# Mamba scan: where the kept state's column is added to the next slot's first column

## The chip, the cores and the metric

One Trainium2 chip, one of its cores. The metric is the device time of one execution in microseconds; several executions are timed and the median is given. The engines named here are TensorE (PE; PEld are its weight loads), VectorE (DVE), ScalarE (ACT), GpSimd (POOL) and SyncE (SP, which issues DMAs). They run side by side, each through its own instructions in order, and wait for one another by semaphores.

## What is computed

The network has two layers on a map of 64 x 64 positions with 256 channels, all in float32: first convolutions with an attention over channels and heads, then a bidirectional Mamba block with a small MLP, then a layer of eight experts of which two are used. The change lies in the Mamba block alone. Cut to it:

```python
# per direction; x: (1, 4096, 256), DI = 512 channels, DS = 16 states
xz = einsum('bld,ed->ble', x, in_proj_w);  xc, z = split(xz, 2)
xc = silu(causal_conv4(xc) + conv_b)
x_dbl = einsum('bld,ed->ble', xc, x_proj_w)      # dt (16), B (16), C (16)
dt = softplus(einsum('blr,dr->bld', dt, dt_proj_w) + dt_proj_b)
A = -exp(A_log)
dA = exp(dt[..., None] * A)                      # decay
dBx = dt[..., None] * Bm[:, :, None, :] * xc[..., None]   # inflow

def step(h, inp):
    dA_t, dBx_t, C_t = inp
    h = dA_t * h + dBx_t                         # 512 x 16 states, position after position
    return h, einsum('bds,bs->bd', h, C_t)

y = (scan(step) + xc * Dp) * silu(z)
return einsum('bld,ed->ble', y, out_proj_w)
```

The block runs forward and on the reversed sequence; the two results are added, and a layer norm with an MLP follows.

## The kernel before

**Phases.** The program runs convolutions, attention, Mamba and experts one after the other (lines 2296 to 2301). The Mamba phase goes from about 1.9 ms to 3.8 ms of the profile.

**Chunks and slots.** The 4096 positions are cut into 8 chunks of N = 512. With two directions that makes 16 passes i (chunk i // 2, direction i % 2; the directions alternate). A pass has SPS = 32 slots: 4 channel tiles e, 4 groups of states k, and j in (0, 2). A slot handles 64 channels times 4 states on 128 partitions (32 channels x 4 states), in two halves v that lie one behind the other in a tile of 128 x 1024. `slots` lists all 512 of them in order (L1871).

**What a slot does.** ScalarE makes the decay dA of both halves into a tile `da` in PSUM (`decay`, L1886, two activations of 512). GpSimd makes the inflow `dbx` in SBUF (`inflow`, L1896). VectorE runs h = dA * h + dBx along all 1024 columns in one instruction (`recur`, L1909), whose first value comes from the kept state, and then multiplies the result by C (L1914). In five slots of a pass (POOLED = 4, 10, 12, 18, 28) the scan writes to SBUF, and GpSimd does that product (`pooled`, L1919). ScalarE copies the last column of each half to the kept state (`keep`, L1940). TensorE sums over the states (`sum_states`, L1949).

**Two halves in one scan.** The second half holds other channels, so what the first half leaves must not run into it. For that the first column of dt of these channels is made huge (L1475), so that the decay there is zero. What their own kept state should have given is added to the first column of the second half of `dbx` instead. `carry` makes these values ahead of time, once for each half of a pass: `brought` = exp(A * dt of the first position) * state (L1493 on GpSimd, L1495 on ScalarE, L1498 on GpSimd; its four parts stand at slots 30, 31, 9 and 11 and the exponentials at 30 and 10). `bring` adds one column of `brought` to one column of `dbx` (128 x 1). The passes i = 0 and 1 start from zero and have nothing to bring, so this concerns 448 slots.

**Who brings.** `bring(n, True)` stands in `inflow` for the slots 1, 9, 17 and 24 of a pass (LONG) and runs on GpSimd (L1932, 56 of them). The others are done by ScalarE (L1934, 392 of them): `bring(n + 1)` stands in the loop ahead of `recur(n)`, behind `decay(n + 1)`. The set `there` keeps a slot from being done twice.

**Order.** The loop over the slots (L1985 to L2047) writes out the order of every engine's instructions by hand (`tc.manual_schedule`); what stands first in the loop stands first in each queue. In the round of slot n: a part of `carry`, `inflow(n + 2)`, `keep(n - 1)`, `decay(n + 1)`, `bring(n + 1)`, `recur(n)`, then loads of later tiles by SyncE, `pooled(n - 1)`, the sums over states, and a step of the work beside it: the next pass's projections (`prepare`), the output projection, and the layer norm and MLP of a finished chunk (`tail`: L1554, L149 on GpSimd; L129, L1568, L1578, L1585 on VectorE). There are three buffers for `dbx`, two for `da` and four for `h`, so GpSimd's inflow of a slot starts when the scan three slots before it has ended.

Of the kernel before, what the change touches and what calls it, by code (L numbers as in the profile page):

```python
# [18 lines left out]
AF = mybir.ActivationFunctionType  # L19
ALU = mybir.AluOpType  # L20
# [41 lines left out]
def step(gen, n=1):  # L62

    for _ in range(n):
        if gen is None or next(gen, StopIteration) is StopIteration:
            return False
    return True
# [1188 lines left out]
def mamba_phase(cx, early, w_in, w_x, w_out, w1, w2, x1d, ud, bcd, dtd, x2d, u2d, usum):  # L1256
# [11 lines left out]
    nc, tc = cx.nc, cx.tc  # L1268
    with ExitStack() as ctx:
# [60 lines left out]
        def exp_and_log():  # L1330
            nc.scalar.preload_act_table_set("natural_log_exp_and_others")
# [153 lines left out]
        def carry(q, h, part):  # L1485


            tiles = slice(2 * h, 2 * h + 2)
            if part == 0:
                x = brought[q, h] = ip.tile([P, 2, 2, SQ], FP, name="brought", tag="in")  # L1490
                first = got_first.pop((q, h)).rearrange("p (a b) e -> p e a b", b=2)[:, :, :, 1]
                a = aneg[q % 2].rearrange("p (e a b k) -> p e a b k", e=ET, a=2, b=2)[:, tiles, :, 1, :]
                nc.gpsimd.tensor_tensor(x, a, first[..., None].to_broadcast([P, 2, 2, SQ]), ALU.mult)  # L1493
            elif part == 1:
                nc.scalar.activation(brought[q, h], brought[q, h], AF.Exp)  # L1495
            else:
                old = state[q % 2].rearrange("p (e a b) k -> p e a b k", a=2, b=2)[:, tiles, :, 1, :]
                nc.gpsimd.tensor_tensor(brought[q, h], brought[q, h], old, ALU.mult)  # L1498
# [367 lines left out]
        def slab(n):  # L1866
# [4 lines left out]
        slots = [  # L1871
            (i, e, k, j) for i in range(2 * NCH) for e in range(ET) for k in range(SQ) for j in (0, 2)
        ]
        SPS = ET * SQ * 2
        firsts, first_rows, got_first, brought = {}, {}, {}, {}
        gots, bcs, dts, m_of, das, us, ys, hs = {}, {}, {}, {}, {}, {}, {}, {}

        def decay(n):

            if n >= len(slots):  # L1880
                return
            i, e, k, j = slots[n]
            da = das[n] = pda.tile([P, 2, N], FP, name="da", tag="da")
            for v in range(2):
                a = SQ * (4 * e + j + v) + k
                nc.scalar.activation(  # L1886
                    da[:, v, :], dts[i, e, j][0][:, v, :], AF.Exp, scale=aneg[i % 2][:, a : a + 1]
                )

        def inflow(n):  # L1890

            if n >= len(slots):
                return
            i, e, k, j = slots[n]
            u = us[n] = up.tile([P, 2, N], FP, name="dbx", tag="dbx")
            nc.gpsimd.tensor_tensor(  # L1896
                u, dts[i, e, j][1], bcs[i, k][0][:, None, :].to_broadcast([P, 2, N]), ALU.mult
            )
            if n % SPS in LONG:
                bring(n, True)  # L1900

        def recur(n):

            i, e, k, j = slots[n]
            da, u = das[n], us.pop(n)
            h = hs[n] = hp.tile([P, 2, N], FP, name="h", tag="h")
            if n % SPS in POOLED:
                das[n] = h
            nc.vector.tensor_tensor_scan(  # L1909
                das[n].rearrange("p v n -> p (v n)"), da.rearrange("p v n -> p (v n)"),  # L1910
                u.rearrange("p v n -> p (v n)"), state[i % 2][:, 4 * e + j, k : k + 1], ALU.mult, ALU.add,
            )
            if n % SPS not in POOLED:
                nc.vector.tensor_tensor(h, da, bcs[i, k][1][:, None, :].to_broadcast([P, 2, N]), ALU.mult)  # L1914

        def pooled(n):

            i, e, k, j = slots[n]
            nc.gpsimd.tensor_tensor(hs[n], hs[n], bcs[i, k][1][:, None, :].to_broadcast([P, 2, N]), ALU.mult)  # L1919

        def bring(n, pool=False):


            if n >= len(slots) or n in there:
                return
            there.add(n)
            i, e, k, j = slots[n]
            if i < 2:
                return
            x, old = us[n][:, 1, 0:1], brought[i, e // 2][:, e % 2, j // 2, k : k + 1]  # L1930
            if pool:
                nc.gpsimd.tensor_tensor(x, x, old, ALU.add)  # L1932
            else:
                nc.scalar.activation(x, x, AF.Identity, bias=old)  # L1934

        def keep(n):

            i, e, k, j = slots[n]
            g = 4 * e + j
            nc.scalar.copy(state[i % 2][:, g : g + 2, k], das.pop(n)[:, :, N - 1])  # L1940
# [16 lines left out]
            g, z = gots[i]["xc"], gots[i]["z"]  # L1957
            nc.vector.tensor_tensor(g[:, e, :], ys.pop((i, e)), z[e // 2][:, e % 2, :], ALU.mult)

        there = set()  # L1960
        CARRY = {30: (0, 0), 31: (0, 2), 9: (1, 0), 11: (1, 2)}


# [2 lines left out]
        AHEAD = 5  # L1966

        LATE = {0: 0, 1: 0, 2: 0, 3: 0, 5: 2, 6: 2, 7: 5, 15: 2, 16: 2, 17: 2}
        LONG = {1, 9, 17, 24}

        FULL = {
            "PE": {0, 1, 2, 3, 4, 5, 6, 7, 9, 18, 19, 20, 21, 23, 24, 25, 27, 29},
# [6 lines left out]
        with tc.manual_schedule(engines=ORDERED):  # L1979
            gots[0] = {"u": early.u}  # L1980
            begin = start()
            step(begin)
            coming = prepare(1)
            tails, prep, out, last = [], None, None, None
            for n, (i, e, k, j) in enumerate(slots):  # L1985
                at = n % SPS
                if at == 0:
                    prep, coming = coming, None
                if at in CARRY and 1 < i + (at > 16) < 2 * NCH:
                    carry(i + (at > 16), *CARRY[at])  # L1990
                inflow(n + 2)
                if n > 0:
                    keep(n - 1)
                if n > 0:
                    decay(n + 1)
                bring(n + 1)
                recur(n)
                nxt = (i, e + 1) if e < ET - 1 else (i + 1, 0)
                if nxt[0] < 2 * NCH:
                    if e == ET - 1 and j == 0:  # L2000
                        load_bc(i + 1, k)
                    if (k, j) == (1, 2):
                        load_dt(*nxt, 0)
                    if (k, j) == (2, 2):
                        load_dt(*nxt, 2)
                if n > 0 and (n - 1) % SPS in POOLED:
                    pooled(n - 1)
                if j == 2 and n > 2 and (n - 3) % SPS in POOLED:
                    sum_states(n - 3)
                if j == 0 and n > 0:  # L2010
                    if (n - 2) % SPS not in POOLED:
                        sum_states(n - 2)
                    if k == 0:
                        close(*slots[n - 2][:2])
                        if e == 0:
                            out = output(i - 1)
                if 1 <= at <= 3 and out is not None:
                    step(out)
                    if at == 3:
                        out = None  # L2020
                        if (i - 1) % 2:
                            tails.append(tail((i - 1) // 2))
                if at == 0 and i > 0:
                    for z in gots[i]["z"]:
                        nc.scalar.activation(z, z, AF.Silu)
                    exp_and_log()
                if i == 0:
                    step(begin)
                step(prep, LATE.get(at, 1) if i == 0 else 1)
                if at >= SPS - AHEAD and i + 2 < 2 * NCH:  # L2030
                    coming = coming or prepare(i + 2)
                    step(coming)
                if i > 0 and at in (2, 4):
                    dt_piece(i, 1, 2 if at == 2 else 3)
                if at == 1 and i > 1:
                    load_first(i, 1)
                elif at in (10, 30) and 1 < i + (at > 16) < 2 * NCH:
                    carry(i + (at > 16), at < 16, 1)
                if i == 2 * NCH - 1 and at in (4, 5, 6, 7, 10, 11, 12, 13, 15, 17, 19, 21, 23, 25, 27, 28, 29, 30):
                    last = last or ahead()  # L2040
                    step(last)
                for _ in range(1 + (i == 2 * NCH - 1 and at in (4, 6, 7))):
                    if tails and (i == 2 * NCH - 1 or at not in FULL[needs[0]]):
                        needs[0] = next(tails[0], None)
                        if needs[0] is None:
                            tails.pop(0)
                            needs[0] = "PE"  # L2047
            ending()
# [357 lines left out]
```

## Time and profile before

| | us |
|---|---|
| median of 3 runs | 4104.75 (4104.18 to 4105.28) |
| the profiled execution | 4093.77 |
| its span, first to last instruction | 4091.8 |
| busy: PE / DVE / ACT / POOL | 3572.0 / 3502.8 / 2628.2 / 1837.9 |
| mean granted clock of TensorE | 0.928 |

The instructions that bring, and those that make what they bring (mean duration, ns):

| line, engine | count | mean | busy us |
|---|---|---|---|
| L1934 ACT, adds the column | 392 | 280 | 109.9 |
| L1932 POOL, adds the column | 56 | 189 | 10.6 |
| L1493 POOL | 28 | 222 | 6.2 |
| L1495 ACT | 28 | 213 | 6.0 |
| L1498 POOL | 28 | 222 | 6.2 |
| L1940 ACT, keeps the state | 511 | 160 to 186 | 83.7 |

How to read the lines of the profile: a group has its line, engine and operation, what it writes and reads by the program's names, shapes (partitions x elements), the count; then busy us and mean ns of one; then the idle time of the engine just before them and what ended most of it. In a timeline the first number is the start in us from the span's start, the second the duration. Starts matter more than durations there: an instruction can start before the one ahead of it on its engine has ended.

### The profile page before, as it was taken

The page shows a single profiled execution, that of the slowest core. Times are in us where ns is not written, and L with a number is a line of the kernel's source. Part 1 is how long each engine was busy: PE and PEld are TensorE (multiplying, and loading weights), DVE is VectorE, ACT ScalarE, POOL GpSimd, SP SyncE. Part 2 cuts the span into 40 slices and gives each one's busy share as a digit, 9 for nine tenths or more (in the row PEclk, how much of TensorE's full clock was granted, in tenths as well). Part 3 has the DMA queues.
Part 4 walks back from the last instruction along what each step waited for, and adds up shares of the span by engine and source line. Part 5 has one row for each costly group of instructions (what it writes and reads, how often), then busy time and mean ns, then how long its engine had stood idle before and what let it go on. Part 6 is the DMA issues. An engine that isn't in the chain of part 4 may idle for free. (4 is left out here: it accounts for less than half of the span.)

```text
span 4091.8 us, 43210 instructions
## 1 busy us (share of the span) xinstructions
PE 3572.0 (87%) x14792; PEld 1173.9 (29%) x14792; DVE 3502.8 (86%) x2919; ACT 2628.2 (64%) x4118; POOL 1837.9 (45%) x1284
## 2 busy tenths in 40 slices
PE   6769988999999999998788888888888888876898
PEld 2324332222222222222222222222222232222444
DVE  8998877989889889877899999999999999999322
ACT  1111236988888888875777777777787777775222
POOL 3020000000000000001888889989888989888100
PEclk9879998999999999998888899999889899888999
DMA  6232214223223222214334444344334444432111
GB/s 209 94 101 92 79 62 152 57 55 71 63 55 65 64 59 61 58 42 126 119 105 130 114 126 132 119 127 122 119 109 122 142 110 133 123 118 93 62 62 55
DMA packets 164324, 399.93 MB, mean 98 GB/s; under 512 B 36997, under 2 KB 46469, under 8 KB 163838
## 3 DMA queue, kind: packets, MB, share of 16 engines
q1 hardware_dynamic: 137166, 304.26, 24.4%
q0 software_dynamic: 24624, 84.43, 8.9%
q10 hardware_dynamic: 2304, 8.39, 0.6%
q8 instruction: 118, 1.93, 0.2%
q14 instruction: 112, 0.92, 0.1%
HBM read 268.17 MB, written 79.56 MB: 85 GB/s over the span
## 5 line engine op out<-in xcount | busy, mean ns | idle before, releaser
L1896 POOL TENSOR_TENSOR dbx<-dtxr,b 128x1024 f32<-128x1024 f32 x512 | 1202.8, 2359 | 192.6 <-DVE da L1909 89.6
L1044 ACT ACTIVATE e<-sc 128x1024 f32<-128x1024 f32 x1024 | 993.8, 1023 | 168.1 <-PE sc L1037 144.0
L1909 DVE TENSOR_TENSOR_SCAN da<-da,state,dbx 128x1024 f32<-128x1024 f32 x432 | 1013.8, 2347 | 16.4 <-ACT da L1886 7.0
L954 DVE TENSOR_TENSOR s<-s,e 128x1024 f32<-128x1024 f32 x768 | 880.2, 1216 | 18.7 <-ACT e L1044 18.0
L1886 ACT ACTIVATE da<-dtr,aneg 128x512 f32<-128x512 f32 x1024 | 708.1, 692 | 33.6 <-DMA dtr<-dtd 3.1
L1037 PE MATMUL sc<-q,kS 32*128 32x512 f32 x4096 | 648.2, 645 | 15.7 <-ACT e L1044 11.4
L1914 DVE TENSOR_TENSOR h<-da,c 128x1024 f32<-128x1024 f32 x432 | 529.0, 1225 | 32.1 <-DVE da L1909 0.5
L961 PE MATMUL av<-e,vT 128*32 128x512 f32 x4096 | 552.3, 608 | 0.1
L977 POOL DMA_DIRECT2D s<-s x94 | 81.5, 874 | 943.4 <-DVE s L954 872.8
L1949 PE MATMUL y<-h,sel 128*32 128x512 f32 x2048 | 374.6, 661 | 96.3 <-DVE h L1914 72.8
L462 PE MATMUL cv<-v,u 128*128 128x512 f32 x928 | 413.8, 606 | 27.5 <-DVE pad L283 14.2
L1037 PEld LDWEIGHTS sc<-q,kS 32*128 32x128 f32 x4096 | 211.2, 184 | 456.1 <-issue 256.2
L1342 PE MATMUL mm<-u,win 128*128 128x512 f32 x464 | 242.8, 665 | 71.2 <-ACT z L1450 30.0
L1940 ACT COPY state<-da 128x2 f32<-128x2 f32 x431 | 68.8, 160 | 292.0 <-DVE h L1914 288.2
L462 PEld LDWEIGHTS cv<-v,u 128*128 128x128 f32 x928 | 179.2, 195 | 260.2 <-issue 227.5
L560 DVE SCALAR_TENSOR_TENSOR acc<-pad,wdw_s,acc 128x768 f32<-128x768 f32 (+1 forms) x192 | 235.9, 1234 | 19.9 <-ACT acc L553 14.2
L143 POOL TENSOR_TENSOR ln_few<-ln_few,minus_half 128x4 f32<-128x4 f32 x29 | 36.2, 1249 | 397.6 <-DMA ln_few<-ln_row 260.2
L1388 PE MATMUL mm<-xp,taps 128*128 128x512 f32 x480 | 213.3, 596 | 0.5 <-DVE m L1538 0.5
L954 DVE TENSOR_TENSOR s<-e 128x1024 f32<-128x1024 f32 x128 | 151.8, 1217 | 60.7 <-ACT e L1044 60.5
L1909 DVE TENSOR_TENSOR_SCAN h<-da,state,dbx 128x1024 f32<-128x1024 f32 x80 | 187.5, 2344 | 10.8 <-ACT state L1940 9.8
L961 PEld LDWEIGHTS av<-e,vT 128*32 128x32 f32 x4096 | 81.9, 108 | 394.3 <-issue 385.9
L1919 POOL TENSOR_TENSOR h<-h,c 128x1024 f32<-128x1024 f32 x80 | 188.4, 2355 | 1.0 <-ACT state L1940 1.0
(375 smaller groups left out, 3887.0 us busy)
## 6 DMA issues: line engine op xcount, KB each, us to landing
dtr<-dtd SPq DMA_DIRECT2D x128, 512.0 KB
dtxr<-dtd SPq DMA_DIRECT2D x128, 512.0 KB
s<-s POOLq DMA_DIRECT2D x94, 512.0 KB, 6.0
b<-bcd SPq DMA_DIRECT2D x64, 256.0 KB
c<-bcd SPq DMA_DIRECT2D x64, 256.0 KB
dtd<-dt SPq DMA_DIRECT2D x64, 256.0 KB
dtd<-few SPq DMA_DIRECT2D x64, 256.0 KB
u<-uv SPq DMA_DIRECT2D x24, 640.0 KB
```

What stands on the lines that cost most here:

```text
L462: nc.tensor.matmul(rows4(ps), u[:, dy, P * ci : P * ci + P], v[:, dy : dy + HR, ci, :], start=dy + ci == 0, stop=dy == k - 1 and ci == CT - 1,
L560: nc.vector.scalar_tensor_tensor(o, src, w_ap, o, ALU.mult, ALU.add)
L954: nc.vector.tensor_tensor(z, x, y, ALU.add)
L961: nc.tensor.matmul(g.av[32 * h : 32 * h + 32, :], vT[:, kb, P * t + 32 * h : P * t + 32 * h + 32], es[h // 2][:, h % 2, :], start=kb == 0, ...
L1037: nc.tensor.matmul(ps[h // 2][:, h % 2, :], kS[r, t, P * kb : P * kb + P], q_t[r, t, :], start=True, stop=True,)
L1044: nc.scalar.activation(e, ps[i], AF.Exp)
L1342: nc.tensor.matmul(ps, win[d][:, t, P * e : P * e + P], u[:, t, ::-1] if d else u[:, t, :], start=t == 0, stop=t == CT - 1,)
L1886: nc.scalar.activation(da[:, v, :], dts[i, e, j][0][:, v, :], AF.Exp, scale=aneg[i % 2][:, a : a + 1])
L1896: nc.gpsimd.tensor_tensor(u, dts[i, e, j][1], bcs[i, k][0][:, None, :].to_broadcast([P, 2, N]), ALU.mult)
L1909: nc.vector.tensor_tensor_scan(das[n].rearrange("p v n -> p (v n)"), da.rearrange("p v n -> p (v n)"), u.rearrange("p v n -> p (v n)"), st ...
L1914: nc.vector.tensor_tensor(h, da, bcs[i, k][1][:, None, :].to_broadcast([P, 2, N]), ALU.mult)
L1949: nc.tensor.matmul(ys[i, e][32 * j : 32 * j + 32, :], cx.sel, hs[n + j // 2][:, j % 2, :], start=False, stop=k == SQ - 1,)
```

## The change

All additions of the kept state's column go to VectorE. `bring(n + 1)` is now called inside `recur(n)`, behind the scan of slot n and ahead of its product, as a tensor_scalar with the column of `brought` as its per-partition scalar. It is no longer called in `inflow` and in the loop; `LONG` and `there` are gone. The passes 0 and 1 are left out as before, now by the number of the slot.

```diff
@@ inflow(n)
                 u, dts[i, e, j][1], bcs[i, k][0][:, None, :].to_broadcast([P, 2, N]), ALU.mult
             )
-            if n % SPS in LONG:
-                bring(n, True)
@@ recur(n)
                 u.rearrange("p v n -> p (v n)"), state[i % 2][:, 4 * e + j, k : k + 1], ALU.mult, ALU.add,
             )
+            bring(n + 1)
             if n % SPS not in POOLED:
                 nc.vector.tensor_tensor(h, da, bcs[i, k][1][:, None, :].to_broadcast([P, 2, N]), ALU.mult)
@@
-        def bring(n, pool=False):
+        def bring(n):
-            if n >= len(slots) or n in there:
+            if n >= len(slots) or n < 2 * SPS:
                 return
-            there.add(n)
             i, e, k, j = slots[n]
-            if i < 2:
-                return
-            x, old = us[n][:, 1, 0:1], brought[i, e // 2][:, e % 2, j // 2, k : k + 1]
-            if pool:
-                nc.gpsimd.tensor_tensor(x, x, old, ALU.add)
-            else:
-                nc.scalar.activation(x, x, AF.Identity, bias=old)
+            x = us[n][:, 1, 0:1]
+            nc.vector.tensor_scalar(x, x, brought[i, e // 2][:, e % 2, j // 2, k : k + 1], None, ALU.add)
@@
-        there = set()
-        LONG = {1, 9, 17, 24}
@@ the loop over the slots
                     decay(n + 1)
-                bring(n + 1)
                 recur(n)
```

## The prediction

> **What bounds the kernel now.** I read the totals of the page first, then the busy time of each engine in the stretch that the change touches (the 448 slots that bring a state, 2165 to 3800 us), then VectorE's waits in it, and then the timeline of VectorE instruction by instruction. These are the groups of the page and the row of the stretch (columns of the second: length, busy us of PE, PEld, DVE, ACT, POOL, clock, DMA):
>
> ```profile
> L1896 POOL TENSOR_TENSOR dbx<-dtxr,b 128x1024 f32<-128x1024 f32 x512 | 1202.8, 2359 | 192.6 <-DVE da L1909 89.6
> L1909 DVE TENSOR_TENSOR_SCAN da<-da,state,dbx 128x1024 f32<-128x1024 f32 x432 | 1013.8, 2347 | 16.4 <-ACT da L1886 7.0
> L1914 DVE TENSOR_TENSOR h<-da,c 128x1024 f32<-128x1024 f32 x432 | 529.0, 1225 | 32.1 <-DVE da L1909 0.5
> ...
> 2165.00:3800.00 1635.00, 1362.22 (x3856) 439.34 (x3856) 1575.77 (x963) 1226.94 (x2431) 1430.72 (x875) 0.90 0.40 119
> ```
>
> VectorE is busy for 1575.8 of 1635 us (96%), GpSimd 88%, TensorE 83%, ScalarE 75%. VectorE sets the pace; each microsecond that it gains or loses here moves everything behind, since the expert phase starts from the last chunk. What it waits for in the stretch (us in total, times, longest):
>
> ```profile
> DVE h L1909 <- ACT state L1940: 9.8, 13, 1.6
> DVE da L1909 <- ACT state L1940: 4.6, 8, 1.0
> DVE da L1909 <- ACT dbx L1934: 3.0, 6, 1.0
> DVE da L1909 <- POOL dbx L1932: 1.0, 1, 1.0
> ```
>
> So the scans lose 18.4 us in 28 places to ScalarE and GpSimd, and only 4.0 of that to the instruction that moves (L1934 and L1932). That is nearly all there is to gain.
>
> **What is removed and added.** ScalarE loses 392 activations (0.28 us each, 109.9 us; it gets back about 0.20 us start to start), GpSimd loses 56 additions (0.19 us, 10.6 us). VectorE gains 448 additions of one column, 378 behind a scan that a product follows, 70 (slots 4, 10, 12, 18, 28 of the 14 later chunks) behind a scan whose product is GpSimd's. No DMA is added or moved. What VectorE's timeline shows between its instructions (start, duration):
>
> ```profile
> 2642.07 2.34 DVE L1909 TENSOR_TENSOR_SCAN h<-da,state,dbx 128x1024 f32<-128x1024 f32 x1
> 2644.33 2.33 DVE L1909 TENSOR_TENSOR_SCAN da<-da,state,dbx 128x1024 f32<-128x1024 f32 x1
> 2646.70 1.23 DVE L1914 TENSOR_TENSOR h<-da,c 128x1024 f32<-128x1024 f32 x1
> 2647.84 2.35 DVE L1909 TENSOR_TENSOR_SCAN da<-da,state,dbx 128x1024 f32<-128x1024 f32 x1
> ```
>
> An instruction that does not need the scan's result starts 2.26 us after the scan's start (2642.07 to 2644.33, before the scan has ended). The product needs the result and starts 2.36 to 2.39 us after it in 182 of the 432 pairs and 2.42 to 2.46 in 249 (2.45 where it has a second semaphore to wait for, as at 2614.16 and 2616.61). So 0.12 to 0.19 us of the pipe are free between scan and product. The price of the new instruction is not in the stretch; its nearest row is a one-element tensor_scalar with a scalar read from SBUF, in the router:
>
> ```profile
> 3837.81 0.15 DVE L2085 TENSOR_SCALAR tw<-slab 128x1 f32<-128x1 f32 x1
> 3837.88 0.20 DVE L2086 TENSOR_SCALAR tw<-tw,slab 128x1 f32<-128x1 f32 x1
> 3838.00 0.86 DVE L169 TENSOR_SCALAR diag<-ident,ln_few 128x128 f32<-128x128 f32 x4
> ```
>
> It lasts 0.20 us, and the next one starts 0.12 after it.
>
> 1. *The 378 slots with a product.* 2.26 + 0.12 = 2.38: the addition fits in front of the product. Cost 0 to 0.12 each, 0 to 45 us; I take 2 us, as sum and row meet almost exactly. The cover is the product's own wait for the scan; without it, the 45 us would show.
>
> 2. *The 70 slots without a product.* Here the next scan reads the column that was just added. In 54 of them it is the next instruction, today 2.26 us after the scan. After the change: addition at 2.26, its end 0.20 later, and the dependent start 0.10 after that (a scan that waits for ScalarE as well has two semaphores, as the product at 2.45). 54 x 0.31 = 16.7 us; bounds 0.24 (one semaphore, 0.034 gap) and 0.12 if nothing waits: 6 to 17. In 16 of them a tail instruction (L129, L1568, L1578) stands between and only the 0.12 counts: 1.9 us.
>
> 3. *The wait that VectorE now takes itself.* The addition needs GpSimd's dbx of the next slot, and stands in VectorE's queue in front of the product, which does not need it; behind the product are the next scan, ScalarE's copy of the state, the decay into the PSUM buffer and TensorE's sums. Before, ScalarE took that wait:
>
> ```profile
> L1934 ACT ACTIVATE dbx<-dbx,brought x392: 277/279/297, 2165.0 to 3792.0; 128x1 f32<-128x1 f32 x196
> ...
>   POOL dbx L1896: 16.0, 23
> ```
>
> 23 times it stood waiting, while VectorE had a 1.14 us product to do. One such place:
>
> ```profile
> 2563.61 2.35 DVE L1909 TENSOR_TENSOR_SCAN da<-da,state,dbx 128x1024 f32<-128x1024 f32 x1
> 2566.07 1.23 DVE L1914 TENSOR_TENSOR h<-da,c 128x1024 f32<-128x1024 f32 x1
> 2567.21 0.74 DVE L1568 SCALAR_TENSOR_TENSOR a1a<-tl,small,a1a 128x512 f32<-128x512 f32 x1
> 2567.97 2.36 DVE L1909 TENSOR_TENSOR_SCAN da<-da,state,dbx 128x1024 f32<-128x1024 f32 x1
> ...
> 2565.26 4.66 POOL L1896 TENSOR_TENSOR dbx<-dtxr,b 128x1024 f32<-128x1024 f32 x2
> ```
>
> The first of GpSimd's two products, for the scan at 2567.97, ends at 2567.60. VectorE would reach the addition at 2563.61 + 2.26 = 2565.87 and stand for 1.77 us; the product moves from 2566.07 to about 2567.76. I compared each slot's scan start + 2.26 with the end of the matching GpSimd product (and of the chunk's L1498): late in 25 places. Neighbours counted once at the longest, and 0.98 us that one scan waits already taken off: 14.6 us. Most lie behind slots 4, 10 and 12, which step 2 makes longer by 0.31 each while GpSimd goes on; that takes off 0.6 to 0.9 in six of them. I take 10 (5 to 15). What is late next is nothing on GpSimd: it waits 76.0 + 15.4 us for scans elsewhere.
>
> 4. *Gains.* The 4.0 us of waits for the moved instruction go. The 21 waits for L1940 (14.4 us) stand behind decays that a ScalarE addition may have delayed by 0.20: at most 4.2, I take 3. GpSimd's 10.6 us lie beside VectorE's work and bring nothing.
>
> Sum: 2 + 16.7 + 1.9 + 10 - 4 - 3 = **+23.6 us**. The profiled execution takes 4093.77 us (span 4091.8, 2.0 around it), so 4117.4; the median of the runs shown, 4104.75, is 11 us (0.27%) above that execution, and I add to the median: **4128 us**.
>
> **A rival of large price: the two engines lock each other out.** One row near the end speaks for it:
>
> ```profile
> 3743.48 2.35 POOL L1896 TENSOR_TENSOR dbx<-dtxr,b 128x1024 f32<-128x1024 f32 x1 [3.17 <-DVE da L1909]
> ...
> 3744.58 0.15 DVE L1718 TENSOR_TENSOR win<-mm,small 128x4 f32<-128x4 f32 x1
> 3744.76 1.09 DVE L1719 TENSOR_SCALAR b1c<-win 128x4 f32<-128x4 f32 x1
> ```
>
> A tensor_scalar of four elements, SBUF to SBUF, lasts 1.09 us in place of about 0.16 and ends at 3745.85, GpSimd's product at 3745.83. L1626 (128x512) does the same: 0.42 us three times, 2.58 while GpSimd works. If the one-element form does this, each addition stands until GpSimd's running instruction ends: at 328 of the 448 points one is running, with 299 us left in sum; with steps 2 and 3 that gives about 4105 + 299 + 26 = 4430 us. Against it: L2086 has just the new form, and ran 0.20 us inside a GpSimd instruction (L2112, 3837.13 to 3838.22), though one that issues a DMA and computes nothing. I go by the row of the same form, and leave 12% to this.
> The Trainium skill states the lock too (SBUF — State Buffer, Who interferes with whom: a VectorE instruction in a two-port mode and GpSimd exclude each other for whole instructions), which L1719 bears out. It also says when that mode is taken (Advanced Engine Details and Errata, 2x-2p Requirements: the outermost dimension even, or odd, above 1 and equal): by that a single element stays out of it and the sum stays as it is; by the lock without this condition it would be 4430. No run here shows a single element beside a GpSimd product.
>
> **Other rivals.** *The addition is not hidden in front of the product* (step 1 at its upper end): it speaks for this that the fit has no room (2.38 against 2.36 to 2.39), against it that 249 products start later than that. 4128 + 43 = 4171 us, 10%.
> *ScalarE was the late one* (the other side): rid of 110 us, it has each decay and state ready in time, all 18.4 us of waits go and GpSimd, 10.6 us freer, is no longer late. Charged with step 2 alone, 4104.75 + 18.6 - 18.4 = 4105 us; from where step 2 costs under 0.15 us a slot (8 us) it turns into a gain of 8 us or more (4096). For it: ScalarE is the last releaser in 27 of the 28 waits. Against it: these waits are up to 1.6 us long and the addition accounts for 0.20. 18%.
>
> **How the numbers follow.** Forecast 60%, not hidden 10%, lock 12%, ScalarE 18%. Time: 4128. About 0.2% (8 us) is what this kernel's runs can tell from no change. Range: from 4100 (the upper part of the ScalarE case) to 4176 (the unhidden case with some room), leaving out the lock and the gains. Slower: forecast, unhidden and lock, 82%, with 2 of the forecast's points ending inside 8 us: 80%. ScalarE's 18%: 12 no change, 6 faster. So faster 6%, same 14%, slower 80%.
>
> **What would show it.** Step 1: scan to product still 2.38 or 2.45 us, scan to the new instruction 2.26. Step 2: scan to scan 2.5 to 2.6 us in slots without a product. Step 3: VectorE waiting for POOL dbx in front of the new instruction, some 10 us, mostly in slots 0, 14 and 15. Step 4: L1934 gone, the waits for L1940 near 12 us. The lock: the new instruction's mean far over 0.20 us. I am wrong if scan to product grows by 0.1 us, or if scan to scan stays at 2.26.

## The result, and the profile after

| | before | after |
|---|---|---|
| median of 6 runs, us | 4104.47 (4095.73 to 4108.36) | 4126.35 (4121.27 to 4130.62) |
| profiled execution, us (span) | 4093.77 (4091.8) | 4121.27 (4119.5) |
| start of scan 63 to start of scan 511, us | 1632.9 | 1661.8 |
| busy from 2165 us to 3800 (before) and 3825 (after): VectorE / ScalarE / GpSimd, us | 1575.8 / 1226.9 / 1430.7 | 1613.4 / 1158.5 / 1421.2 |

The change makes the kernel slower: ratio 1.0054, 95% interval 1.0041 to 1.0067, that is 17 to 27 us. 4128 was forecast. The third row of the table is used below as a ruler. It takes the scans' starts from the timeline, so it holds the 448 slots that bring and nothing else. What lies ahead of scan 63 took between 2151.8 and 2169.4 us in the kernels of this study without any edit there, which is more than most of the effects.

The page's groups after, and the row of the stretch (scan is now L1907, product L1913):

```profile
L1896 POOL TENSOR_TENSOR dbx<-dtxr,b 128x1024 f32<-128x1024 f32 x512 | 1201.4, 2358 | 232.8 <-DMA dtxr<-dtd 89.3
L1907 DVE TENSOR_TENSOR_SCAN da<-da,state,dbx 128x1024 f32<-128x1024 f32 x432 | 1015.3, 2350 | 21.5 <-ACT da L1886 9.9
L1913 DVE TENSOR_TENSOR h<-da,c 128x1024 f32<-128x1024 f32 x432 | 528.9, 1224 | 5.2
...
2165.00:3825.00 1660.00, 1383.44 (x3850) 444.62 (x3851) 1613.37 (x1408) 1158.45 (x2037) 1421.15 (x819) 0.89 0.40 118
```

Scan and product cost what they did. The idle time in front of the product went from 32.1 to 5.2 us: the new instruction now stands there. The new group, and what VectorE waits for in the stretch:

```profile
L1927 DVE TENSOR_SCALAR dbx<-dbx,brought 128x1 f32<-128x1 f32 x448 | 85.2, 190 | 11.4 <-POOL dbx L1896 10.7 <-POOL brought L1498 0.7
...
DVE xc L1951 <- PE y L1942: 14.4, 7, 2.9
DVE dbx L1927 <- POOL dbx L1896: 10.7, 14, 2.0
DVE h L1907 <- ACT da L1886: 8.0, 8, 1.4
DVE da L1907 <- ACT da L1886: 2.5, 9, 0.8
DVE dbx L1927 <- POOL brought L1498: 0.7, 1, 0.7
```

The group's durations come to 85.2 us, but the stretch grew by only 28.9 us, because most of them lie inside time that was there. VectorE's timeline shows both kinds of slot:

```profile
2651.43 2.34 DVE L1907 TENSOR_TENSOR_SCAN h<-da,state,dbx 128x1024 f32<-128x1024 f32 x1
2653.69 0.19 DVE L1927 TENSOR_SCALAR dbx<-dbx,brought 128x1 f32<-128x1 f32 x1
2653.98 2.36 DVE L1907 TENSOR_TENSOR_SCAN da<-da,state,dbx 128x1024 f32<-128x1024 f32 x1
2656.25 0.19 DVE L1927 TENSOR_SCALAR dbx<-dbx,brought 128x1 f32<-128x1 f32 x1
2656.38 1.23 DVE L1913 TENSOR_TENSOR h<-da,c 128x1024 f32<-128x1024 f32 x1
2657.51 2.35 DVE L1907 TENSOR_TENSOR_SCAN da<-da,state,dbx 128x1024 f32<-128x1024 f32 x1
2659.77 0.19 DVE L1927 TENSOR_SCALAR dbx<-dbx,brought 128x1 f32<-128x1 f32 x1
2659.95 1.22 DVE L1913 TENSOR_TENSOR h<-da,c 128x1024 f32<-128x1024 f32 x1
```

With a product: scan at 2653.98, product at 2656.38 (2.40 later), and at 2657.51 and 2659.95 (2.44), as before; the addition starts 2.26 after the scan. Without one: scan at 2651.43, next scan at 2653.98, 2.55 in place of 2.26.

The third loss is where GpSimd is late: 15 places, 10 of them in slots 14 and 15, 4 in slot 0 and 1 in slot 31. One of them:

```profile
2807.31 2.35 DVE L1907 TENSOR_TENSOR_SCAN da<-da,state,dbx 128x1024 f32<-128x1024 f32 x1
2810.67 0.21 DVE L1927 TENSOR_SCALAR dbx<-dbx,brought 128x1 f32<-128x1 f32 x1 [1.02 <-POOL dbx L1896]
2810.80 1.21 DVE L1913 TENSOR_TENSOR h<-da,c 128x1024 f32<-128x1024 f32 x1
2811.93 0.74 DVE L1568 SCALAR_TENSOR_TENSOR a1a<-tl,small,a1a 128x512 f32<-128x512 f32 x1
2812.59 2.35 DVE L1907 TENSOR_TENSOR_SCAN da<-da,state,dbx 128x1024 f32<-128x1024 f32 x1
```

The addition stands 1.02 us in front of a product and of L1568, which needed nothing of it; the product starts 3.49 us after its scan.

Slot by slot (interval from scan to scan, after less before, summed over the 14 passes) the 28.9 us are: +17.7 in the five slots without a product, +5.3 in slots 14 and 15, +6.5 in slot 16, +2.6 in slot 0, +1.6 in slot 31, -4.4 in slot 1, -1.2 in slot 9, and within 0.7 in every other slot. In slots 20 to 27, where every addition stands in front of a product and nothing is late, no single interval differs by more than 0.01 us.

### The profile page after: what moved, and what is told of

Read it like the earlier page. It is cut to its first block, busy times and chain, and to the rows that moved or that the text cites. A ratio compares the mean times of both kernels' runs of the same rounds, so it can differ in the third digit from the quotient of the medians.

```text
span 4119.5 us, 43727 instructions
## 1 busy us (share of the span) xinstructions
PE 3589.0 (87%) x14792; PEld 1178.6 (29%) x14792; DVE 3538.7 (86%) x3367; ACT 2561.8 (62%) x3726; POOL 1825.6 (44%) x1228
## 5 line engine op out<-in xcount | busy, mean ns | idle before, releaser
L1907 DVE TENSOR_TENSOR_SCAN da<-da,state,dbx 128x1024 f32<-128x1024 f32 x432 | 1015.3, 2350 | 21.5 <-ACT da L1886 9.9
L1886 ACT ACTIVATE da<-dtr,aneg 128x512 f32<-128x512 f32 x1024 | 708.1, 692 | 35.0 <-DMA dtr<-dtd 4.4
L1037 PE MATMUL sc<-q,kS 32*128 32x512 f32 x4096 | 646.7, 644 | 16.7 <-ACT e L1044 11.4
L1913 DVE TENSOR_TENSOR h<-da,c 128x1024 f32<-128x1024 f32 x432 | 528.9, 1224 | 5.2
L1942 PE MATMUL y<-h,sel 128*32 128x512 f32 x2048 | 388.3, 667 | 95.7 <-DVE h L1913 69.7
L462 PE MATMUL cv<-v,u 128*128 128x512 f32 x928 | 415.1, 608 | 28.9 <-DVE pad L283 14.3
L1907 DVE TENSOR_TENSOR_SCAN h<-da,state,dbx 128x1024 f32<-128x1024 f32 x80 | 187.5, 2344 | 10.9 <-ACT da L1886 8.6
```

Of the source, the lines that this page charges most:

```text
L462: nc.tensor.matmul(rows4(ps), u[:, dy, P * ci : P * ci + P], v[:, dy : dy + HR, ci, :], start=dy + ci == 0, stop=dy == k - 1 and ci == CT - 1,
L1037: nc.tensor.matmul(ps[h // 2][:, h % 2, :], kS[r, t, P * kb : P * kb + P], q_t[r, t, :], start=True, stop=True,)
L1886: nc.scalar.activation(da[:, v, :], dts[i, e, j][0][:, v, :], AF.Exp, scale=aneg[i % 2][:, a : a + 1])
L1907: nc.vector.tensor_tensor_scan(das[n].rearrange("p v n -> p (v n)"), da.rearrange("p v n -> p (v n)"), u.rearrange("p v n -> p (v n)"), st ...
L1942: nc.tensor.matmul(ys[i, e][32 * j : 32 * j + 32, :], cx.sel, hs[n + j // 2][:, j % 2, :], start=False, stop=k == SQ - 1,)
```

## The experiments

Two theories. *Place*: an addition between scan and product is free; the loss is in the slots where the next scan reads it at once, in VectorE's own wait for GpSimd, and in what that wait delays. *Uniform*: 448 more instructions on the busiest engine cost some 0.06 us each. Every kernel below is the changed one with an edit.

| kernel | median | ratio to before (95%) | stretch | VectorE's waits in it: GpSimd, TensorE's y, ScalarE |
|---|---|---|---|---|
| before | | 1 | 1632.9 | 1.0, 8.0, 17.7 |
| after | 4126.35 | 1.0054 (1.0041 to 1.0067) | 1661.8 | 11.4, 14.4, 10.5 |
| e1, no additions | 4095.91 | 0.998 (0.9968 to 0.9993) | 1626.0 | 0.9, 5.3, 13.0 |
| e2, behind the product | 4207.3 | 1.0256 (1.0235 to 1.0277) | 1742.0 | 0, 13.2, 10.9 |
| e3, two columns | 4280.47 | 1.0434 (1.0406 to 1.0462) | 1819.5 | 2.1, 10.8, 9.3 |
| e4, after pooled scans by ScalarE | 4109.93 | 1.0024 (1.0011 to 1.0037) | 1642.9 | 13.0, 9.2, 11.7 |
| e5, late slots by ScalarE | 4112.54 | 1.0042 (1.0026 to 1.0058) | 1650.2 | 0, 10.9, 11.2 |
| e6, both | 4092.82 | 0.9989 (0.998 to 0.9998) | 1625.9 | 0.9, 1.2, 13.8 |
| e7, after pooled scans by GpSimd | 4114.99 | 1.0038 (1.0025 to 1.0051) | 1644.7 | 13.4, 9.0, 11.0 |

Each ratio is to runs of the kernel before on the same chip (medians there 4099.46 for e1 to e4 and 4097.48 for e5 to e7), so ratios are compared, not medians. Stretch and waits are those of one profiled execution of each kernel. The waits are of over some 0.12 us: for GpSimd those in front of the addition or the scan, for y those in front of the product that closes a channel tile (xc), for ScalarE those in front of the scans.

**e1: what all of it costs.**

```diff
-            bring(n + 1)
```

> The changed kernel without the 448 additions: the kept state's column is not added at all (that part of the computation is left out). Place theory (the additions are hidden in front of a product and cost only in the 54 slots where the next scan reads the column, in 16 where a tail instruction follows, and where VectorE waits for GpSimd's dbx): against the changed kernel it loses 16.0 + 1.6 + 11.4 us and the 6.5 us of TensorE waits of slot 16, so about 4126 - 35 = 4091 us, ratio to the kernel before 0.995 to 0.999; scan to product unchanged at 2.38 and 2.45 us. Uniform theory (each addition takes some 0.06 us of VectorE): about 4126 - 27 = 4099, and scan to product shorter by 0.05 us than in the changed kernel.

The ratio 0.998 lies in the range of the place theory, but its interval holds uniform's 4099 too (0.9987); the stretch and the timeline decide. In the stretch the changed kernel's additions cost 35.8 us (1661.8 to 1626.0), where place said 35.5 and uniform 27. Scan to product has a median of 2.44 us without and 2.45 with the addition, so what uniform asked for (0.05) is not there. It also prices the kernel before: there the same additions on ScalarE and GpSimd cost 6.9 us.

**e2: the free place.**

```diff
-            bring(n + 1)
             if n % SPS not in POOLED:
                 nc.vector.tensor_tensor(h, da, ...)
+            bring(n + 1)
```

> The addition stands behind the product in place of between scan and product. Place theory: the next scan reads the column in every slot, so product to scan grows from 1.14 to about 1.44 us in the 378 slots with a product: 378 x 0.30 = 113 us more, less some 10 us of waits for GpSimd that fall away (1.2 us more time for it): 4126 + 103 = 4229 us, ratio to before 1.025 to 1.032. Uniform theory: same number of instructions, same time as the changed kernel, 1.005.

The same 448 instructions, 80 us slower than the changed kernel in the stretch. VectorE's timeline of this kernel:

```profile
2650.71 0.20 DVE L1927 TENSOR_SCALAR dbx<-dbx,brought 128x1 f32<-128x1 f32 x1
2651.02 2.36 DVE L1907 TENSOR_TENSOR_SCAN da<-da,state,dbx 128x1024 f32<-128x1024 f32 x1
2653.48 1.23 DVE L1912 TENSOR_TENSOR h<-da,c 128x1024 f32<-128x1024 f32 x1
2654.62 0.20 DVE L1927 TENSOR_SCALAR dbx<-dbx,brought 128x1 f32<-128x1 f32 x1
2654.74 0.74 DVE L1568 SCALAR_TENSOR_TENSOR a1b<-tl,small,a1b 128x512 f32<-128x512 f32 x1
```

A scan that reads the column starts 0.31 after the addition (2650.71 to 2651.02), an instruction that does not read it 0.12 after it (2654.62 to 2654.74). The expectation was 20 us too high, as it took all 378 slots for direct ones; the scan follows the addition directly in 272, something else does in the others. Uniform, which had the same time as the changed kernel, falls.

**e3: the lock.**

```diff
-            x = us[n][:, 1, 0:1]
+            x = us[n][:, 1, 0:2]
```

> Each addition covers two columns in place of one (the second column gets the addend too, which the computation does not ask for). If an even count makes VectorE and GpSimd lock each other out, as the 4-element row L1719 of the kernel before showed, and one element stays out of it: the additions' mean goes from 0.19 us to about 0.8, many end within 0.05 us of the end of a GpSimd product, and the time grows by 250 to 355 us, to 4380 to 4480 us. If the lock has nothing to do with the count: as the changed kernel, 4126 us, 0.19 us each.

The group of the additions, and one of them in VectorE's timeline of this kernel:

```profile
L1927 DVE TENSOR_SCALAR dbx<-dbx,brought 128x2 f32<-128x2 f32 x448 | 271.5, 606 | 2.1 <-POOL dbx L1896 1.8 <-POOL brought L1498 0.3
...
2637.98 2.34 DVE L1927 TENSOR_SCALAR dbx<-dbx,brought 128x2 f32<-128x2 f32 x1
```

GpSimd's timeline beside it:

```profile
2637.95 2.35 POOL L1918 TENSOR_TENSOR h<-h,c 128x1024 f32<-128x1024 f32 x1
```

The addition starts 0.03 us after GpSimd's product and ends 0.02 after its end (2640.32 and 2640.30). 162 of the 448 additions last over 0.25 us, 1.32 on average, and all 162 end within 0.06 us of the end of a GpSimd instruction. With one column, 310 of the 448 start while GpSimd is in an instruction, last 0.19 us, and none is longer than 0.22. So the lock is real and one element stays out of it. The size was put too high (250 to 355): the stretch grew by 158 us. With two columns only 208 additions start while GpSimd is in an instruction.

**e4, e7: the slots behind a scan without a product.** A table says who brings which slot, and `bring` is called at the three places with the engine's name.

```diff
+        BY = {5: "ACT", 11: "ACT", 13: "ACT", 19: "ACT", 29: "ACT"}
...
+            if ... or by != BY.get(n % SPS, "DVE"):
+                return
...
+                bring(n + 1, "ACT")
                 recur(n)
```

> The changed kernel, but the additions of slots 5, 11, 13, 19 and 29 (those behind a scan without a product; 70 of 448) are ScalarE's again, ahead of recur as before. Place theory: scan to scan back from 2.56 to 2.26 us in 54 slots and 0.10 less in 16, 17.6 us, less up to 3 us of waits for ScalarE that come back: 4126 - 16 = 4110 us, ratio to before 1.000 to 1.003. Uniform theory: 70 x 0.06 = 4 us, 4122. ScalarE theory (the loss is elsewhere and ScalarE's relief is what holds it down): 4126 or more.

18.9 us less than the changed kernel in the stretch, ratio 1.0024: place, not uniform (4). Slot by slot, 15.2 us of it are in the five slots themselves; slot 16 lost 5.3 more, which the expectation did not have, and slots 14 and 15 grew by 3.3. VectorE's timeline of e4 has scan to scan back at 2.26 us:

```profile
2643.38 2.35 DVE L1908 TENSOR_TENSOR_SCAN h<-da,state,dbx 128x1024 f32<-128x1024 f32 x1
2645.64 2.33 DVE L1908 TENSOR_TENSOR_SCAN da<-da,state,dbx 128x1024 f32<-128x1024 f32 x1
```

e7 has "POOL" in the table, called behind the inflow.

> As the run with slots 5, 11, 13, 19 and 29 by ScalarE, but by GpSimd, right behind its inflow of that slot. Place theory: VectorE gains the same 17.6 us, GpSimd gets 70 x 0.19 = 13 us more, of which what lies ahead of its late products (the slots 11 and 13 of a pass, 28 x 0.19 = 5 us) makes VectorE wait longer: 4126 - 13 = 4113 us, ratio to before 1.001 to 1.004. Uniform theory: 4122.

17.1 us less in the stretch, and the waits for GpSimd grow from 11.4 to 13.4, 2 us in place of 5.

**e5: the late slots.**

```diff
+        BY = {0: "ACT", 15: "ACT", 16: "ACT", 1: "POOL"}
```

> The changed kernel, but the additions of slots 0, 15 and 16 are ScalarE's and that of slot 1 is GpSimd's (56 of 448), so that VectorE does not itself wait in the slots where GpSimd's dbx came late (0, 14, 15, 31). Place theory: the 11.4 us that VectorE waited in front of the addition go; the product of slot 15 is in time again and with it TensorE's sums, so that the 6.5 us more of waits in slot 16 (VectorE for TensorE's y) go as well; the gains of about 4 us in slot 1 may be given back. 4126 - 15 = 4111 us, ratio to before 1.000 to 1.004. Rival (the waits of slot 16 come from elsewhere): 4126 - 9 = 4117 us and slot 16 keeps its waits. Uniform theory: 56 x 0.06 = 3 us, 4123.

VectorE's waits for GpSimd are gone (11.4 to 0) and the stretch is 11.6 us shorter, where uniform asked for 3. But the waits for TensorE only went from 14.4 to 10.9, so the rival was right in part: in slot 16 TensorE's matmuls (L1562) start in time again, 4.39 us after the scan of slot 15 in all six odd passes (5.42 in five of six after), and VectorE still waits 1.35 to 2.2 us for y. The ratio alone (1.0042 against 1.0054, intervals overlapping) does not tell; what e5 shows rests on the stretch and the waits of one profiled execution.

**e6: both, and a better kernel.**

```diff
+        BY = {0: "ACT", 5: "ACT", 11: "ACT", 13: "ACT", 15: "ACT", 16: "ACT", 19: "ACT", 29: "ACT", 1: "POOL"}
```

> Both: slots 0, 5, 11, 13, 15, 16, 19 and 29 by ScalarE, slot 1 by GpSimd, the other 23 of a pass by VectorE between scan and product (322 of 448). Place theory: only the hidden additions are left on VectorE, and ScalarE still has about 280 activations less than before: 4126 - 17 - 15 = 4094 us, down to the kernel before or up to 10 us faster than it, ratio 0.9965 to 1.0005. Uniform theory: 322 x 0.06 = 19 us above before, ratio 1.004 to 1.005.

VectorE keeps 322 additions, all in front of a product. The stretch (1625.9) is as short as with no additions at all (1626.0), 7 us shorter than before; the ratio is 0.9989, interval 0.998 to 0.9998, so it beats the kernel before by 0.8 to 8 us. Slot by slot the 7 us are all in slot 16 (6.8 less than before); the other slots together are within 0.3 us of before. VectorE's waits for y are nearly gone there (14.4 after, 1.2 here), more than e4 and e5 together would give (5.2 and 3.5 of 13.2). The granted clock goes with it. TensorE's weight loads of slot 16 of one pass, after, and the row of that window (length, busy us of PE, PEld, DVE, ACT, POOL, then the granted clock and the DMA):

```profile
2812.73 0.50 PEld L1562 LDWEIGHTS tl<-hn,w1s 128*128 128x128 f32 x2 [4.20 <-DVE a1a L1568]
2813.74 0.34 PEld L1562 LDWEIGHTS tl<-hn,w1s 128*128 128x128 f32 x1 [0.52 <-issue]
...
2812.60:2816.30 3.70, 3.57 (x4) 1.17 (x4) 3.66 (x4) 2.87 (x3) 3.70 (x3) 0.50 0.00 0
```

and in e6:

```profile
2801.93 0.30 PEld L1562 LDWEIGHTS tl<-hn,w1s 128*128 128x128 f32 x2 [2.31 <-DVE a1a L1568]
2802.47 0.19 PEld L1562 LDWEIGHTS tl<-hn,w1s 128*128 128x128 f32 x1 [0.24 <-issue]
...
2801.80:2803.80 2.00, 1.87 (x4) 0.68 (x4) 1.78 (x2) 1.97 (x5) 2.00 (x1) 1.00 0.00 0
```

The four matmuls behind L1568 start 0.85 to 1.01 us apart after, 0.43 to 0.53 in e6; the clock granted in these windows is 0.50 and 1.00. The sums y stand behind them in TensorE's queue, and VectorE waits for y at the end of slot 16. L1562 stands in slot 16 of the six odd passes 3 to 13; in all eleven kernels that makes 66 places. Take the mean clock from the start of the first of these matmuls to the start of the fourth. In the 48 places where it was 0.50 to 0.59, VectorE then waited 0.94 to 3.7 us; in the 12 where it was 1.00, not at all. In the six between (0.65 to 0.71) it waited 0 to 0.2 us four times, 0.7 once (e3) and 2.5 once (e8). After, the clock was 0.50 in all six passes; before, 0.50 in three and 0.58 in one; in e6, 1.00 in five and 0.66 in one.

**e8 and e9: does the clock cause it?** Both give TensorE more to do ahead of slot 15.

```diff
                     ps = mm_psum()
-                    nc.tensor.matmul(ps, wdt[...], xd[r, :], start=True, stop=True)
+                    for _ in range(4):              # e9: 1 + (e > 1)
+                        nc.tensor.matmul(ps, wdt[...], xd[r, :], start=True, stop=True)
```

> The changed kernel with each matmul of the dt projection (L1418, slots 11 to 14 of a pass) issued four times into the same place instead of once, so that TensorE has more to do ahead of slot 15 (360 matmuls more, which only repeat the same result). Clock theory (VectorE's wait for TensorE's y in slot 16, 14.4 us in the changed kernel, comes from TensorE running the four L1562 matmuls of that slot at a granted clock of 0.50, after little work in slots 13 to 15): these four run at 1.00 in most of the odd passes, the waits in slot 16 fall below 7 us, and the stretch from scan 63 to scan 511 shrinks from 1661.8 us by 5 to 9. Order theory (the sums are late because the work in front of them is released late, whatever the clock): clock or not, the waits stay at 12 us or grow, as TensorE has more to do.

4329.33 us, ratio 1.0563 (1.0535 to 1.0591). The four matmuls of slot 16 stayed at 0.50 to 0.65 and TensorE itself became the limit in slots 14 to 16 (VectorE waited 77.2 us for y in front of products alone). It tells nothing of the clock.

> As the run with four matmuls, but only the last two of the four tiles e of the dt projection (slots 13 and 14) are issued, and those twice: 60 matmuls more in place of 360. Clock theory: some of the four L1562 matmuls of slot 16 of the odd passes run at 1.00 in place of 0.50, and where they do, VectorE's wait for y in that slot is under 0.3 us; where the clock stays at 0.50 it is 1 to 2.2 us. Order theory: the waits of slot 16 do not go with the clock, and grow by the time of the added matmuls. If all stay at 0.50, the test says nothing.

Ratio 1.0104 (1.007 to 1.0139), slower than the changed kernel's 1.0054, though the stretch of its profiled execution, the fastest of the four, is 1663.8, only 2 us from the changed kernel's; the difference is not explained. One of the six places (slot 16 of pass 3) went up to a clock of 1.00, and its wait from 2.2 to 0.0 us; five stayed at 0.50 to 0.53 with 1.9 to 2.2. That fits the clock theory, but it is one place, and no edit raised the clock and left the rest.

Two passes of e1 come nearest to that. In slot 16 of passes 7 and 9 the same four matmuls start 4.39 us after the scan of slot 15, behind the same 1.44 us in which TensorE stood still; the clock granted in them was 1.00 in pass 7 (2804.15 to 2805.54) and 0.50 in pass 9 (3035.95 to 3038.66). From VectorE's and TensorE's timelines of e1:

```profile
2799.76 2.35 DVE L1907 TENSOR_TENSOR_SCAN da<-da,state,dbx 128x1024 f32<-128x1024 f32 x1
2804.02 2.35 DVE L1907 TENSOR_TENSOR_SCAN da<-da,state,dbx 128x1024 f32<-128x1024 f32 x1
2804.15 1.98 PE L1562 MATMUL tl<-hn,w1s 128*128 128x512 f32 x4 [1.44 <-DVE a1a L1568]
2807.61 0.68 DVE L1950 TENSOR_TENSOR xc<-y,z 128x512 f32<-128x512 f32 x1
...
3031.56 2.35 DVE L1907 TENSOR_TENSOR_SCAN da<-da,state,dbx 128x1024 f32<-128x1024 f32 x1
3035.81 2.35 DVE L1907 TENSOR_TENSOR_SCAN da<-da,state,dbx 128x1024 f32<-128x1024 f32 x1
3035.95 3.78 PE L1562 MATMUL tl<-hn,w1s 128*128 128x512 f32 x4 [1.44 <-DVE a1a L1568]
3041.66 0.69 DVE L1950 TENSOR_TENSOR xc<-y,z 128x512 f32<-128x512 f32 x1 [2.17 <-PE y L1941]
```

At 1.00 VectorE does not wait for y, at 0.50 it waits 2.17 us with everything in front at the same distance. So in this pair the clock makes the wait, and late work does not. What sets the clock is another question. After, it was 0.50 already for 14.4 us ahead of the matmuls of pass 5 (likewise in passes 9 and 13), and 1.00 until 3.0 us ahead of those of pass 7:

```profile
2560.50:2574.90 14.40, 11.51 (x24) 2.57 (x24) 12.95 (x13) 11.03 (x21) 14.40 (x7) 0.50 0.61 197
2806.30:2809.60 3.30, 2.29 (x11) 0.45 (x10) 3.30 (x2) 2.80 (x6) 3.30 (x2) 1.00 0.76 271
```

In pass 11 it fell as in pass 7, inside the idle time in front of the matmuls; in pass 3 too, where no addition was late. So the late product can have brought the half clock on in two of the six places at most, and why these kernels differ in it stays open.

## Why the prediction was right

It forecast +23.6 us; the medians moved by 21.9, the two profiled executions by 27.5, the stretch by 28.9. Term by term, in the stretch:

| step of the prediction | forecast, us | measured, us |
|---|---|---|
| 1: additions in front of a product | 2 (0 to 45) | about 1; scan to product 2.44 to 2.45 |
| 2: next scan reads it, 54 slots and 16 | 16.7 + 1.9 | 17.7; 0.29 each in the 54, 0.10 in the 16 |
| 3: VectorE waits for GpSimd itself | 10 | 11.4, in 15 places, 10 of them slots 14 and 15 |
| 4: waits in front of the scans that go | -7 | -7.7 (18.7 to 11.0, 0.5 of it behind VectorE's own addition) |
| VectorE's waits for TensorE's y | not in the sum | +6.4 (8.0 to 14.4) |

Steps 1 to 3 stand: step 1 by e1 and by slots 20 to 27, step 2 by e4 and e7, step 3 by e5. Step 4 is read from the waits alone: the 14.4 us for L1940, forecast at near 12, are 10.5 us after, put down to the decay L1886.

What the sum lacks is VectorE's wait for TensorE's y. Its row stands in the view of before from which the prediction took its list of waits, and the list leaves it out (9.0 us up to 3800, 8.0 up to scan 511):

```profile
DVE xc L1958 <- PE y L1949: 9.0, 6, 2.0
```

So the 18.4 us in front of the scans were not "nearly all there is to gain"; e6 gained on before in slot 16, where VectorE waits for y. And the last sentence of step 3, having named TensorE's sums among what is queued behind the product, says that nothing is late next, looking at GpSimd alone. After, five of the six slots 15 passed the product and L1568 on 1 us later, TensorE's weight loads of slot 16 stood idle 3.8 to 4.7 us in place of 1.7 to 2.5, its next matmuls ran at half the clock in all six, and the close of the channel tile waited: 11.5 us in these six places in place of 6.7. That the late product caused the half clock is not shown (e8 and e9 above, and e5, which is in time and at 0.50). The total came out near the forecast in spite of this term; part of the agreement of the medians to 2 us is luck, as the interval is 10 us wide and the stretch moved by 5 us more than was forecast.

The rivals: the lock does not touch one element (12% was given to it; e3, with two, shows what it costs there, +158 us in the stretch, where 302 was written). "Not hidden" falls by the scan-to-product times of e1 and after. "ScalarE was the late one" was half a mechanism: the waits for ScalarE did shrink, from 17.7 to 10.5 us after and to 13.8 in e6, but e6's gain on before is in slot 16, not there.

## What to carry to other kernels

An engine that is busy 96% of the time can still have room for a small instruction: between two long ones of which the second needs the first's result. Such a place is worth the gap between "next independent" and "next dependent" start (here 2.26 and 2.38 to 2.45 us), and nothing when the small one's own reader comes next. Before a wait is moved to the busiest engine, look at which of its instructions would stand behind it, and put every row of its waits into the sum, those for engines that the change does not touch too; hand the few late cases to an engine that has time.

## What the runs showed of the hardware

A one-element tensor_scalar in SBUF runs beside GpSimd's instructions untouched (310 of them, 0.19 us), a two-element one is held until GpSimd's instruction ends (162, 1.32 us on average). The Trainium skill's condition for the two-port mode (Advanced Engine Details and Errata, 2x-2p Requirements) agrees on both sides.

The granted clock of TensorE took two values in these matmuls, 1.00 and 0.50 (0.52 to 0.71 on the mean where it changed between the first and the fourth); no other value stands in the clock records of the eleven traces. The Trainium skill (TensorE: Matmul & The Clock Gate, What's actually happening) has the half clock follow an idle window of some 3.4 us. These traces neither bear that out nor refute it: after, TensorE's matmuls stood still 2.1 to 3.8 us in front of slot 16's, but in three of six passes the half clock was 14 us old by then. In pass 5 the matmul records follow one another without a gap from 2561.37 to 2572.89 (their ends are modelled), and the clock stayed at 0.50 throughout. e5 was at 0.50 with its weight loads idle for 2.3 to 3.1 us in front, and those some 8 us ahead were slow already (0.34 us for one in place of 0.19).
